# Rows of four tokens per partition, D x made in the merge, and the next B and C loaded between batches, in a four-layer selective-scan and FFT network

## The chip, the cores and the metric

The kernel runs on one core of a Trainium2 chip, as one launch that holds a whole four-layer network. The metric is the device time of one execution in microseconds (us). Everything in the network is in 32-bit floats but a part of the feed-forward layers, which this change does not touch.

## What is computed

The input x is an image batch of (4, 64, 64, 96): four images, 4096 tokens each, 96 channels. Four layers follow one another, each adding to a running x. Layers 0 and 1 are selective state-space layers over images ("SS2D"), and they hold the change; layers 2 (linear attention and a feed-forward part) and 3 (a filter in the frequency domain and a feed-forward part) do not take part in it. Layer 0, cut to what matters:

```
xz = gn(x) @ in_proj_w.T;  xc, z = split(xz)             # 192 channels each
xc = silu(depthwise_conv3x3(xc))
idx, inv = scan orders                                    # four orders of the 4096 tokens
xs = [xc in the order idx[k] for k in 0..3]
dt, B, C = projections of xs[k];  delta = softplus(dt)
h_t = h_(t-1) * exp(delta_t * A) + delta_t * u_t * B_t    # 16 states for each channel
y_t = sum over states of h_t * C_t
out_y = y + Ds[k] * xs[k]
y_restored = [out_y[k] in the order inv[k]]
w = softmax(small net on each token's position)           # one weight per token and order
y = sum_k w[k] * y_restored[k]
y = layernorm(y) * silu(z);  return y @ out_proj_w.T
```

Layer 1 has the same core with four fixed directions (rows, columns, and both backwards) and no weights w, so that its D terms are a plain sum over k; a feed-forward part follows it. "D x" below is the term of Ds times x summed over the four orders, with the weights w in layer 0.

## The kernel before, in words

**Stages.** The class `Stream` (lines 312 to 1089) does layer 0 and the scans of layer 1. It works on eight batches in turn, q = 0 to 7: the four images of layer 0 ("L0"), then the four of layer 1 ("L1"). A batch has 16 segments: four orders (kd = 0 to 3) of 4096 tokens, cut into four pieces of 1024. A segment has 24 groups, six blocks of 32 channels (cb) by four groups of four states (sg); a group lays 32 channels x 4 states on the 128 partitions, and 1024 tokens along the free axis.

**The scan**, `run`, lines 989 to 1084. The order of its instructions is written out by hand, two groups to a slot. For a group, DVE multiplies u by B (`enter`, L893) and runs the recurrence (`recur`, L900); POOL multiplies the states by C (`leave`, L910); PE sums the states into y (`collect`, L921); ACT makes the decays exp(delta A) (`decay`, L888). u is spread over the partitions by PE (`spread_u`, L880) into a single PSUM buffer, once for each cb. B and C of a segment lie in the tile `bc`, filled by eight loads of 512 KB from DRAM (`load_states`, L865); the loads for the segment that follows are issued in the last two slots of a segment, as its tile parts come free. The delta rows of a cb come by `load_dt` (L871). Beside the groups, the next segment is prepared in small steps (`prepare`, lines 761 to 859), which a helper, `Weave`, places between the PE and ACT work of the slots.

**From channels to tokens.** After each odd cb the y of 64 channels and 1024 tokens is turned (`turn`, lines 955 to 987): four PE transposes of 128x128 (L962), then an ACT copy (L965), three times a segment. In these transposes `yc` is the stationary operand, loaded by a weight load, and the identity moves. When the third is done the segment's rows go to the DRAM tensor `y_tok` of that kd: by eight indirect stores of POOL in the scan order (L974; L0, kd 0 and 1), by one store of SP (L983; L0, kd 2 and 3, and L1, even kd), or by two strided stores of SP (L986; L1, odd kd). Partition p then holds token p of each 128, so that one row of 192 channels, 768 bytes, is contiguous in DRAM.

**Between batches**, `side_by_side` (lines 678 to 706) writes out two stages together: the `merge` of the batch before and the `front` of a batch to come: in the seam ahead of batch q, the merge of q-1 and the front of q+1. Both are written as threads (generators) that name an engine and an assumed time before each step; `Plan` (lines 146 to 198) puts the steps in the order in which a simple model would start them, "ahead" being a priority. `Rings` (lines 204 to 224) say how many buffers of a tile there are: a thread waits till one has been given back. This fixes the order on each engine's queue. SP takes its DMAs strictly in order, and so does POOL with its gathers and multiplications; a DMA that must wait for its tile holds all that are queued behind it.

- *front* (lines 351 to 535): loads of x (L369) and its halo (L381), group norm, the input projection (L429, L445), the convolution on PE in four strips of 1024 tokens (L482), Silu (L494); then 12 transposes a strip (L509; `xc` is stationary) and ACT copies (L512) give `y_rows`, which SP stores as `x_tok` (L520). POOL multiplies the rows by D's weights, in L0 a table by token, `weight_x`, loaded from DRAM by L502, in L1 one row (L523 and L525, 128x1536 elements), and SP stores the product as `dx_tok` (L529). The product's tile, `sp_z`, has one buffer.
- *merge* (lines 538 to 676): for each of eight chunks of 512 tokens, loads of y of the four kd (SP L575; POOL gathers L580 for kd 2 and 3 of L0, four a chunk and kd), a load of `dx` (L550, one buffer), DVE sums (L603 in L0 with w, L607 in L1), statistics (L617, L618), normalisation (L625 to L630), eight transposes back to channels (L638) into one PSUM buffer, ACT's scale and shift (L647), DVE's multiplication by z (L651); then in L0 the output projection (L663) and the new x (L668, L672), in L1 the store of y (L657).

The start does two fronts without a merge. Ahead of q=7 the seam has a merge alone, and after q=7 there is a last merge alone.

Of the kernel before, what the change touches and what calls it, by code (L numbers as in the profile page):

```python
# [23 lines left out]
L = HW * HW  # L24
# [215 lines left out]
class Layer:  # L240


    def __init__(self, s, a, pre, x_in):
# [35 lines left out]
        if self.ordered:  # L279
            self.weight_x = k.t(s.dram, [L, DI], pre + "weight_x", bufs=1)  # L280
            ds = k.load(s.seg, a[pre + "Ds"], "ds")
            for c in range(NCH):
                turned = k.t(s.ps, [ND, CH], "m")
                for j in range(CH // 128):
                    nc.tensor.transpose(
                        turned[:, j * 128 : (j + 1) * 128], s.fuse[:, c * (CH // 128) + j, :], k.ident
                    )
                part = k.t(s.core, [ND, CH], "h", bufs=4)
                nc.vector.tensor_copy(part, turned)
                ps = k.t(s.ps_t, [128, 2, CH], "t")  # L290
# [10 lines left out]
                nc.sync.dma_start(  # L301
                    self.weight_x[c * CH : (c + 1) * CH, :].rearrange("(j p) d -> p j d", p=128),
                    rows.rearrange("p a (b d) -> p (a b) d", d=DI),
                )
        else:
            ds = k.t(s.core, [128, ND, DI], "h", bufs=4)
            nc.sync.dma_start(ds, a[pre + "Ds"].unsqueeze(0).to_broadcast([128, ND, DI]))
            self.weight_x = k.t(w, [128, DI], pre + "weight_x")
            nc.vector.tensor_reduce(self.weight_x, ds.rearrange("p k d -> p d k"), AX.X, ALU.add)


class Stream:
# [38 lines left out]
    def front(self, bt, plan, rings, first=None):  # L351
# [7 lines left out]
        bt.x_tok = k.t(self.dram, [L, DI], "x_tok")  # L359
        bt.dx_tok = k.t(self.dram, [L, DI], "dx_tok", bufs=3)  # L360
# [105 lines left out]
        def convolve(s, st):  # L466
# [30 lines left out]
            to = lambda v: v[s * SEG : (s + 1) * SEG, :].rearrange("(j p) d -> p j d", p=128)  # L497
            dx = yield from take(self.seg, [128, 2, SEG], "sp_z", 1)
            dxs = dx.rearrange("p h t -> p (h t)")[:, : SEG // 128 * DI].rearrange("p (j d) -> p j d", d=DI)
            if lay.ordered:  # L500
                yield "SP", 0.1
                nc.sync.dma_start(dxs, to(lay.weight_x))  # L502
            rows = yield from take(self.tmp, [128, 2, 4, DI], "y_rows", 1)
            two = yield from take(self.ps_t, [128, 2, CH], "t", 2)
            one = yield from take(self.ps, [128, CH], "m", 1)
            for blk, ps in enumerate((two[:, 0, :], two[:, 1, :], one)):
                yield "PE", 1.2
                for t in range(4):
                    nc.tensor.transpose(ps[:, t * 128 : (t + 1) * 128], xc[blk][:, t * 128 : (t + 1) * 128], k.ident)  # L509
                yield "ACT", 0.8  # L510
                for half in range(2):
                    nc.scalar.copy(  # L512
                        rows[:, :, :, half * C + blk * GC : half * C + (blk + 1) * GC],
                        ps.rearrange("p (t h j d) -> p h j t d", h=2, j=2, d=GC)[:, half],
                    )
            give(two, one, *xc)
            del two, one, ps, xc
            flat = rows.rearrange("p j t d -> p (j t) d")
            yield "SP", 0.1
            nc.sync.dma_start(to(bt.x_tok), flat)  # L520
            yield "POOL", 3.5
            if lay.ordered:
                nc.gpsimd.tensor_mul(dxs, dxs, flat)  # L523
            else:
                nc.gpsimd.tensor_mul(dxs, flat, lay.weight_x.unsqueeze(1).to_broadcast([128, SEG // 128, DI]))  # L525
            give(rows)
            del rows, flat
            yield "SP", 0.1
            nc.sync.dma_start(to(bt.dx_tok), dxs)  # L529
            yield "none", 2.5  # L530
            give(dx)
            del dx, dxs
# [5 lines left out]
    def merge(self, bt, plan, rings):  # L538
# [1 line left out]
        k, nc, tmp, lay = self.k, self.nc, self.tmp, bt.lay  # L540
        take, give = rings.take, rings.give
        T = CH // 128
        rows_of = lambda v, n: v[n * CH : (n + 1) * CH, :].rearrange("(j p) d -> p j d", p=128)
        cols_of = lambda n: slice(n * CH, (n + 1) * CH)
        got = {}

# [13 lines left out]
        rings.parts("rows", [whole[:, i, : T * DI].rearrange("p (j d) -> p j d", d=DI) for i in range(2)])  # L560
        whole = k.t(self.seg, [C, 2, SEG], "xs")
        rings.parts("z", [whole[:, i].rearrange("p (h t) -> p h t", h=2) for i in range(2)])

        def fetch(kds):
            if kds[0]:
# [22 lines left out]

        def sums():
            for n in range(NCH):  # L590
                plan.add(load(("dx", n), tmp, [128, T, DI], "dx", 1, rows_of(bt.dx_tok, n)))
            for n in range(NCH):
                acc = yield from take(self.core, [128, T, DI], "hc", 3)
                yield lambda: ("dx", n) in got
# [27 lines left out]
        def finish(n, acc, mv):  # L622
# [21 lines left out]
            yield "ACT", 1.4  # L644
            for half in range(2):
                g, b = lay.ln_g[:, half : half + 1], lay.ln_b[:, half : half + 1]
                nc.scalar.activation(yt[:, half], ps[:, half], AF.Identity, bias=b, scale=g)  # L647
            yield lambda: ("z", n) in got
            z = got.pop(("z", n))
            yield "DVE", 1.1  # L650
# [24 lines left out]

        yield from plan.together([fetch((0, 1)), fetch((2, 3)), sums()])

    def side_by_side(self, ahead, behind=None, flush=None):


        k, nc = self.k, self.nc
        plan, rings = Plan(), Rings(k)
        self.ended, self.idle = False, None

        def ending():

            yield "none", 1.2
            if flush:
                flush()
            self.idle = k.t(self.ps_y, [128, CH], "y")  # L690
            self.ended = True
            yield "PE", 4.0

        def fill():
            if self.idle is not None:
                data = self.layers[0].diag.rearrange("p h t c -> p (h t c)")[:, :384]
                nc.tensor.matmul(self.idle[:GC, :384], self.zeros, data, start=True, stop=True)

        plan.fill = fill
        if behind:  # L700
# [254 lines left out]
    def turn(self, seg, pair, yc):  # L955

        k, nc = self.k, self.nc
        if pair == 0:
            seg.rows = self.spare()[:, : SEG // 128 * DI].rearrange("p (f t d) -> p f t d", f=2, d=DI)
        ps = k.t(self.ps, [128, CH // 128, 128], "m")  # L960
        for j in range(CH // 128):
            nc.tensor.transpose(ps[:, j, :], yc[:, j * 128 : (j + 1) * 128], k.ident)  # L962
        self.put += 0.66
        yield
        nc.scalar.copy(seg.rows[:, :, :, pair * 64 : (pair + 1) * 64], ps.rearrange("p j (f d) -> p f j d", f=2))  # L965
        if pair == 2:
# [13 lines left out]
                    )  # L980
            elif seg.bt.lay.ordered or seg.kd % 2 == 0:
                at = self.start(seg)
                nc.sync.dma_start(to[at : at + SEG, :].rearrange("(j p) d -> p j d", p=128), rows)  # L983
            else:
                for w in range(2):
                    nc.sync.dma_start(self.by_columns(to, seg, w), rows[w * HW : (w + 1) * HW])  # L986
# [2 lines left out]
    def run(self):  # L989
# [15 lines left out]
        with k.tc.manual_schedule():  # L1005
# [16 lines left out]

            for n, (seg, cb, sg) in enumerate(slots):
                follows = seg.next
                if first_of(slots[n]):
                    q = batches.index(seg.bt)
                    if q:
                        self.side_by_side(batches[q + 1 : q + 2], batches[q - 1], flush)
                    before = []
                    seg.bt.y_tok = [k.t(self.dram, [L, DI], f"y_tok{kd}") for kd in range(ND)]  # L1030
                    self.spread_u(seg, 0)
# [41 lines left out]
                if cb == NCB - 1 and follows:  # L1073
# [3 lines left out]
                if cb == NCB - 1 and follows:  # L1077
# [14 lines left out]
def fusion_weights(k, s, a, fuse):  # L1092
# [871 lines left out]

def constants():
    c = {}
    for name, order in zip(("scan_idx", "scan_inv"), scan_orders()):
        c[name] = order.reshape(ND, L // 128, 128).transpose(2, 0, 1).astype(np.uint32)
# [4 lines left out]
    c["coords"] = np.stack([r.ravel(), (np.arctan2(dy, dx) / f(math.pi)).ravel()])  # L1973

    one = np.kron(np.eye(GC), np.ones((1, GS)))
    c["spread"] = np.tile(one, (C // GC, 1))
# [105 lines left out]
```

## Time and profile before

| | |
|---|---|
| median of 3 runs | 16010.31 us (16001.02 to 16012.46) |
| the profiled execution | 15991.09 us |
| its span, first to last instruction | 15989.3 us, mean granted PE clock 0.87 |
| scans and seams (`Stream`) | to about 12,880 us of the span |
| start, to the first enter | 395.4 us |
| seams ahead of q = 1 to 7 (last leave to first enter) | 174.9, 173.7, 174.5, 178.6, 164.5, 162.9, 101.0 us |
| last merge | about 104 us, from 12,776 |
| one batch | 1356 (the last) to 1425 us (the first) |

The page of the profile gives, for each engine, its busy time; then the span in 40 slices, each digit a busy share in tenths; the DMA queues; the chain of work that ended last; and groups of instructions, each with its line, its engine, the tiles it writes and reads, its count, busy time, mean duration, and the idle time of its engine ahead of it with what ended that idle time. A window is a stretch of the span for which the same busy times are asked. PEld is PE's loading of weights, which lies beside its matmuls; SPq lines are DMAs that SP issues, with the time at which each issue began. The trace also has each DMA packet with its size and time; the DMA share is the busy time of the packets over that of the core's 16 DMA engines.

### The profile page before, as it was taken

To read this page: it belongs to the slowest core of one execution; us is meant where nothing else is said; L and a number is where in the kernel's file an instruction comes from. 1 tells how busy PE (TensorE), PEld (TensorE's weight loads), DVE (VectorE), ACT (ScalarE), POOL (GpSimd) and SP (SyncE) were. 2 spreads that over 40 slices of the span, in tenths; PEclk is the share of its full clock that TensorE was granted. 3 is DMA by queue.
4 is the path that set the end of the run, shared out by engine and by line. 5 is a ranking of instruction groups with operands and counts; after the bars stand their busy time and mean duration, and the time that the engine had idled before them with its cause. 6 is when DMAs were issued, how large, how long until landed. Compare 5 with 4: busy or idle time off the path is not lost. (4 is left out here: it accounts for less than half of the span.)

```text
span 15989.3 us, 190160 instructions
## 1 busy us (share of the span) xinstructions
PE 13629.1 (85%) x70689; PEld 4868.9 (30%) x70689; DVE 12884.4 (81%) x9642; ACT 8295.0 (52%) x14192; POOL 9763.9 (61%) x4881
## 2 busy tenths in 40 slices
PE   7888888888888888888878887888888879998877
PEld 3222322232222222222222222222222234443344
DVE  1989798979897989799979997999899965565555
ACT  3656465646564656465555555656466522332334
POOL 0788688868886888677747774777577720000123
PEclk8888888888888888888888888888888889998878
DMA  3333533353335333533353334333433320000132
GB/s 98 113 105 119 161 106 104 118 162 105 113 110 153 107 114 108 154 109 118 106 151 120 105 119 150 111 115 108 145 110 121 104 65 18 18 11 14 39 82 70
DMA packets 883162, 1662.26 MB, mean 104 GB/s; under 512 B 103078, under 2 KB 551339, under 8 KB 878460
## 3 DMA queue, kind: packets, MB, share of 16 engines
q1 hardware_dynamic: 845372, 1574.54, 31.8%
q0 software_dynamic: 36864, 75.55, 1.6%
q8 instruction: 560, 9.18, 0.2%
q14 instruction: 366, 3.00, 0.1%
HBM read 1295.03 MB, written 354.75 MB: 103 GB/s over the span
## 5 line engine op out<-in xcount | busy, mean ns | idle before, releaser
L910 POOL TENSOR_TENSOR hc<-h,bc 128x1024 f32<-128x1024 f32 x3072 | 7186.2, 2358 | 2386.9 <-DVE h L900 1935.1
L900 DVE TENSOR_TENSOR_SCAN h<-da,state,t 128x1024 f32<-128x1024 f32 x2304 | 5271.0, 2328 | 14.1 <-ACT da L888 10.5
L921 PE MATMUL y<-hc,gather_y 128*32 128x512 f32 x12288 | 4295.0, 691 | 700.2 <-POOL hc L910 534.5
L893 DVE TENSOR_TENSOR t<-u,bc 128x1024 f32<-128x1024 f32 x3072 | 3599.8, 1217 | 1023.0 <-PE u L880 899.4
L888 ACT ACTIVATE da<-dts,L_A_logs 128x1024 f32<-128x1024 f32 x3072 | 3487.8, 1147 | 746.2 <-DMA dts<-dt_dram 476.1
L880 PE MATMUL u<-dtu,spread 32*128 32x512 f32 x3072 | 1897.9, 745 | 377.8 <-DVE t L893 370.4
L944 PE MATMUL y<-L_diag,zeros 96*32 96x256 f32 x5218 | 1747.8, 465 | 0.0
L900 DVE TENSOR_TENSOR_SCAN h<-da,t 128x1024 f32<-128x1024 f32 x768 | 1711.8, 2268 | 17.6 <-ACT da L888 16.8
L921 PEld LDWEIGHTS y<-hc,gather_y 128*32 128x32 f32 x12288 | 804.3, 117 | 2499.8 <-issue 1280.2
L849 ACT COPY dt<-m 96x512 f32<-96x512 f32 x512 | 297.1, 580 | 1588.1 <-PE m L844 1588.1
L812 PE MATMUL m<-xs,proj 96*128 96x512 f32 (+1 forms) x2048 | 1016.8, 619 | 115.9 <-ACT dt L821 62.7
L880 PEld LDWEIGHTS u<-dtu,spread 32*128 32x128 f32 x3072 | 603.7, 217 | 1460.0 <-issue 1106.8
L944 PEld LDWEIGHTS y<-L_diag,zeros 96*32 96x32 f32 x5218 | 617.4, 132 | 1283.6 <-issue 1156.4
L1265 POOL MEMSET padp<- 128x2448 f32 x32 | 68.6, 2144 | 1481.9 <-PE d L1305 1376.1
L1341 DVE SCALAR_TENSOR_TENSOR hcv<-padv,taps,hcv 128x2048 f32<-128x2048 f32 x384 | 902.2, 2350 | 13.4
L1305 PE MATMUL d<-padp,diag 32*32 32x512 f32 x25600 | 885.7, 601 | 2.0 <-ACT hcp L1320 2.0
L844 PE MATMUL m<-sp_z,ident 96*96 96x512 f32 x1024 | 534.9, 604 | 190.1 <-ACT sp_z L838 189.9
L804 POOL TENSOR_TENSOR dtu<-sp_z,dtu 96x1024 f32<-96x1024 f32 x256 | 604.2, 2360 | 72.6 <-ACT dtu L802 70.2
L816 ACT ACTIVATE sp_z<-m,L_dtb 96x512 f32<-96x512 f32 x512 | 349.3, 682 | 544.4 <-PE m L812 529.5
L1305 PEld LDWEIGHTS d<-padp,diag 32*32 32x32 f32 x25600 | 483.5, 103 | 370.6 <-issue 197.9
L965 ACT COPY spare<-m 128x512 f32<-128x512 f32 x384 | 225.4, 587 | 706.3 <-PE m L962 706.3
L812 PEld LDWEIGHTS m<-xs,proj 96*128 96x128 f32 (+1 forms) x2048 | 321.8, 177 | 821.9 <-issue 314.8
(275 smaller groups left out, 15523.6 us busy)
## 6 DMA issues: line engine op xcount, KB each, us to landing
bc<-bc_dram SPq DMA_DIRECT2D x1024, 512.0 KB
dts<-dt_dram SPq DMA_DIRECT2D x768, 512.0 KB
dt_dram<-dt SPq DMA_DIRECT2D x256, 384.0 KB
y_tok<-spare SPq DMA_DIRECT2D x64, 768.0 KB
dt<-y_tok SPq DMA_DIRECT2D x128, 384.0 KB
z_t<-z_rows SPq DMA_DIRECT2D x64, 384.0 KB
x_tok<-y_rows SPq DMA_DIRECT2D x32, 768.0 KB
dx_tok<-sp_z SPq DMA_DIRECT2D x32, 768.0 KB
```

The lines of the kernel that those rows point to most:

```text
L804: rest = lambda half: nc.gpsimd.tensor_add(r[:, half], z[:, half], r[:, half])
L812: nc.tensor.matmul(ps, proj[:, src, to], xs[:, src, cols], start=src == 0, stop=src == 1)
L844: nc.tensor.matmul(ps, k.ident[:C, :C], term[:, half, cols], start=at == 0, stop=at == 2)
L880: self.nc.tensor.matmul(seg.u[:, cols], self.spread[rows, :], seg.dtu[rows, half, cols], start=True, stop=True)
L888: self.nc.scalar.activation(da, seg.dts[cb], AF.Exp, scale=seg.bt.lay.neg_a[:, seg.kd, g : g + 1])
L893: self.nc.vector.tensor_mul(gr.t, gr.seg.u, self.bc[:, 0, gr.sg, :])
L900: self.nc.vector.tensor_tensor_scan(gr.h[:, order], gr.da[:, order], gr.t[:, order], start, op0=ALU.mult, op1=ALU.add)
L910: self.nc.gpsimd.tensor_mul(gr.hc, gr.h, self.bc[:, 1, gr.sg, :])
L921: nc.tensor.matmul(seg.y[at : at + GC, :], self.gather_y, gr.hc[:, part * CH : (part + 1) * CH], start=gr.sg == 0, stop=gr.sg == NSG - 1, ...
L944: self.nc.tensor.matmul(gr.seg.y[at : at + GC, :256], self.zeros, gr.seg.bt.lay.diag.rearrange("p h t c -> p (h t c)")[:, :256], start=Fal ...
L1305: nc.tensor.matmul(pc[i][j * 32 : (j + 1) * 32, :], diag[mine, ON_PE.index(t), tap, :], pad[mine, j * 8 + dy : j * 8 + dy + 8, dx : dx + H ...
L1341: nc.vector.scalar_tensor_tensor(to, win, wt, to, op0=ALU.mult, op1=ALU.add)
```

## The change

There are three parts. Line numbers here are those of the kernel before.

1. *Rows of fours.* Partition p holds the four tokens 4p to 4p+3 of each 512 instead of token p of each 128. For this the transposes take every fourth column of their operand (L509 always; L962 in L0, and in L1 for even kd), and the stores and loads of `weight_x`, `x_tok` and `y_tok` in that layout are of 3072 contiguous bytes to a partition instead of four times 768. The constants for the orders and the positions are permuted to match. When the merge turns chunks back to channels, ACT's L647 reads PSUM in the permuted order and writes in the plain one. The strided stores of L1's odd kd and the loads of `x_tok` for the scans (`fetch`) stay as they are.
2. *D x in the merge.* The front no longer loads `weight_x`, multiplies, or stores `dx_tok`. The merge loads `x_tok` where it loaded `dx_tok`, in L0 also `weight_x`, and POOL multiplies the two, a chunk of 128x768 at a time, ahead of the sums. `x_tok` now has three DRAM buffers.
3. *B and C late.* The eight loads of `bc` and the first of the delta rows for a new batch are no longer issued in the last slots of the batch before, but by a thread of the seam, `states`: the first after 50 of the plan's us, the others 4 apart.

```diff
             for blk, ps in enumerate((two[:, 0, :], two[:, 1, :], one)):
                 yield "PE", 1.2
                 for t in range(4):
-                    nc.tensor.transpose(ps[:, t * 128 : (t + 1) * 128], xc[blk][:, t * 128 : (t + 1) * 128], k.ident)
+                    nc.tensor.transpose(ps[:, t * 128 : (t + 1) * 128], xc[blk][:, t::4], k.ident)
...
-            if lay.ordered:
-                yield "SP", 0.1
-                nc.sync.dma_start(dxs, to(lay.weight_x))
...
+            to = bt.x_tok[s * SEG : (s + 1) * SEG, :].rearrange("(j p t) d -> p j (t d)", j=2, t=4)
             yield "SP", 0.1
-            nc.sync.dma_start(to(bt.x_tok), flat)
-            yield "POOL", 3.5
-            if lay.ordered:
-                nc.gpsimd.tensor_mul(dxs, dxs, flat)
-            else:
-                nc.gpsimd.tensor_mul(dxs, flat, lay.weight_x.unsqueeze(1).to_broadcast([128, SEG // 128, DI]))
+            nc.sync.dma_start(to, rows.rearrange("p j t d -> p j (t d)"))
...
-            nc.sync.dma_start(to(bt.dx_tok), dxs)
...
-        rows_of = lambda v, n: v[n * CH : (n + 1) * CH, :].rearrange("(j p) d -> p j d", p=128)
+        rows_of = lambda v, n: v[n * CH : (n + 1) * CH, :].rearrange("(p j) d -> p j d", j=T)
...
+        def times_d(n):
+            x = yield from take(tmp, [128, T, DI], "dx", 1)
+            yield "SP", 0.1
+            nc.sync.dma_start(x, rows_of(bt.x_tok, n))
+            weight = lay.weight_x
+            if lay.ordered:
+                weight = yield from take(None, None, "weight", 2)
+                nc.sync.dma_start(weight, rows_of(lay.weight_x, n))
+            yield "none", 3.0
+            yield "POOL", 1.8
+            if lay.ordered:
+                nc.gpsimd.tensor_mul(x, x, weight)
+                give(weight)
+            else:
+                nc.gpsimd.tensor_mul(x, x, weight.unsqueeze(1).to_broadcast([128, T, DI]))
+            got["dx", n] = x
...
             for n in range(NCH):
-                plan.add(load(("dx", n), tmp, [128, T, DI], "dx", 1, rows_of(bt.dx_tok, n)))
+                plan.add(times_d(n), 1)
...
-                nc.scalar.activation(yt[:, half], ps[:, half], AF.Identity, bias=b, scale=g)
+                to, v = yt[:, half].rearrange("c (p j) -> c p j", j=T), ps[:, half].rearrange("c (j p) -> c p j", j=T)
+                nc.scalar.activation(to, v, AF.Identity, bias=b, scale=g)
...
+        def states():
+            for at in range(2 * NSG):
+                yield "none", 50.0 if at == 0 else 4.0
+                yield "SP", 0.1
+                self.load_states(seg, *divmod(at, NSG))
+            self.load_dt(seg, 0)
...
+        fours = seg.bt.lay.ordered or seg.kd % 2 == 0
         for j in range(CH // 128):
-            nc.tensor.transpose(ps[:, j, :], yc[:, j * 128 : (j + 1) * 128], k.ident)
+            v = yc[:, j::4] if fours else yc[:, j * 128 : (j + 1) * 128]
+            nc.tensor.transpose(ps[:, j, :], v, k.ident)
...
-                nc.sync.dma_start(to[at : at + SEG, :].rearrange("(j p) d -> p j d", p=128), rows)
+                to = to[at : at + SEG, :].rearrange("(f p t) d -> p f (t d)", f=2, t=4)
+                nc.sync.dma_start(to, seg.rows.rearrange("p f t d -> p f (t d)"))
...
                 follows = seg.next
+                near = follows and follows.bt is seg.bt
...
-                        self.side_by_side(batches[q + 1 : q + 2], batches[q - 1], flush)
+                        self.side_by_side(batches[q + 1 : q + 2], batches[q - 1], flush, seg)
...
-                elif sg == 0 and follows:
+                elif sg == 0 and near:
                     self.load_dt(follows, 0)
...
-                    if cb == NCB - 1 and follows:
+                    if cb == NCB - 1 and near:
                         self.load_states(follows, 0, gr.sg)
```

More of the change, by code (lines that the diff above doesn't have):

```diff
@@ L301, in __init__ @@
                 nc.sync.dma_start(
-                    self.weight_x[c * CH : (c + 1) * CH, :].rearrange("(j p) d -> p j d", p=128),
-                    rows.rearrange("p a (b d) -> p (a b) d", d=DI),
+                    self.weight_x[c * CH : (c + 1) * CH, :].rearrange("(p j) d -> p (j d)", j=4),
+                    rows.rearrange("p a e -> p (a e)"),
                 )
@@ L358, in front @@
         x = lay.x_in[:, bt.b, :]
-        bt.x_tok = k.t(self.dram, [L, DI], "x_tok")
-        bt.dx_tok = k.t(self.dram, [L, DI], "dx_tok", bufs=3)
+        bt.x_tok = k.t(self.dram, [L, DI], "x_tok", bufs=3)
         bt.z_t = k.t(self.dram, [C, 2, L], "z_t", bufs=3)
@@ L496, in convolve @@
             del two, one, ps
-            to = lambda v: v[s * SEG : (s + 1) * SEG, :].rearrange("(j p) d -> p j d", p=128)
-            dx = yield from take(self.seg, [128, 2, SEG], "sp_z", 1)
-            dxs = dx.rearrange("p h t -> p (h t)")[:, : SEG // 128 * DI].rearrange("p (j d) -> p j d", d=DI)
-            if lay.ordered:
-                yield "SP", 0.1
-                nc.sync.dma_start(dxs, to(lay.weight_x))
             rows = yield from take(self.tmp, [128, 2, 4, DI], "y_rows", 1)
@@ L517, in convolve @@
             del two, one, ps, xc
-            flat = rows.rearrange("p j t d -> p (j t) d")
+            to = bt.x_tok[s * SEG : (s + 1) * SEG, :].rearrange("(j p t) d -> p j (t d)", j=2, t=4)
             yield "SP", 0.1
-            nc.sync.dma_start(to(bt.x_tok), flat)
-            yield "POOL", 3.5
-            if lay.ordered:
-                nc.gpsimd.tensor_mul(dxs, dxs, flat)
-            else:
-                nc.gpsimd.tensor_mul(dxs, flat, lay.weight_x.unsqueeze(1).to_broadcast([128, SEG // 128, DI]))
-            give(rows)
[L527 to L532, printed above, removed]
+            nc.sync.dma_start(to, rows.rearrange("p j t d -> p j (t d)"))
+            yield "none", 2.5
+            give(rows)
+            del rows
         works = [work for s, st in enumerate(strips) for work in (project(s, st), convolve(s, st))]
@@ L562, in merge @@
         rings.parts("z", [whole[:, i].rearrange("p (h t) -> p h t", h=2) for i in range(2)])
+        whole = k.t(self.seg, [128, 2, SEG], "sp_z")
+        rings.parts("weight", [whole[:, i, : T * DI].rearrange("p (j d) -> p j d", d=DI) for i in range(2)])
+        def times_d(n):
[14 more added lines that the diff above has]
+            got["dx", n] = x
         def fetch(kds):
@@ L676, in merge, with side_by_side @@
         yield from plan.together([fetch((0, 1)), fetch((2, 3)), sums()])
-    def side_by_side(self, ahead, behind=None, flush=None):
+    def side_by_side(self, ahead, behind=None, flush=None, seg=None):
         k, nc = self.k, self.nc
@@ L697, in fill @@
                 nc.tensor.matmul(self.idle[:GC, :384], self.zeros, data, start=True, stop=True)
+        def states():
[4 more added lines that the diff above has]
+            self.load_dt(seg, 0)
         plan.fill = fill
+        if seg:
+            plan.add(states())
         if behind:
@@ L1072, in run @@
                 self.leave(now[0])
-                if cb == NCB - 1 and follows:
+                if cb == NCB - 1 and near:
                     self.load_states(follows, 1, now[0].sg)
@@ L1076, in run @@
                 self.leave(now[1])
-                if cb == NCB - 1 and follows:
+                if cb == NCB - 1 and near:
                     self.load_states(follows, 1, now[1].sg)
@@ L1966, in constants @@
     c = {}
-    for name, order in zip(("scan_idx", "scan_inv"), scan_orders()):
-        c[name] = order.reshape(ND, L // 128, 128).transpose(2, 0, 1).astype(np.uint32)
+    idx, inv = scan_orders()
+    tiles = lambda v: v.reshape(-1, L // 128, 128).transpose(2, 0, 1)
+    fours = lambda v: v.reshape(-1, NCH, 128, 4).transpose(2, 0, 1, 3).reshape(128, -1, L // 128)
+    c["scan_idx"] = np.concatenate([fours(idx[:2]), tiles(idx[2:])], axis=1).astype(np.uint32)
+    c["scan_inv"] = fours(inv).astype(np.uint32)
     f = np.float32
@@ L1972, in constants @@
     r = np.minimum(np.sqrt(dy**2 + dx**2), f(2.0))
-    c["coords"] = np.stack([r.ravel(), (np.arctan2(dy, dx) / f(math.pi)).ravel()])
+    coords = np.stack([r.ravel(), (np.arctan2(dy, dx) / f(math.pi)).ravel()])
+    c["coords"] = coords.reshape(2, NCH, 128, 4).swapaxes(2, 3).reshape(2, L)
     one = np.kron(np.eye(GC), np.ones((1, GS)))
```

## Prediction

> **What bounds the kernel now.** I read the totals first, then the slices of the span, then the costliest groups, then windows cut at the seams between batches.
>
> ```profile
> PE 13629.1 (85%) x70689; PEld 4868.9 (30%) x70689; DVE 12884.4 (81%) x9642; ACT 8295.0 (52%) x14192; POOL 9763.9 (61%) x4881
> ...
> DVE  1989798979897989799979997999899965565555
> ...
> DMA  3333533353335333533353334333433320000132
> ...
> L900 DVE TENSOR_TENSOR_SCAN h<-da,state,t 128x1024 f32<-128x1024 f32 x2304 | 5271.0, 2328 | 14.1 <-ACT da L888 10.5
> ...
> L893 DVE TENSOR_TENSOR t<-u,bc 128x1024 f32<-128x1024 f32 x3072 | 3599.8, 1217 | 1023.0 <-PE u L880 899.4
> ```
>
> The 81% of DVE is a mean over two regimes. Slices 1 to 32 are the scans (to about 12,880 us): DVE has 8s and 9s, with a dip wherever the DMA row rises to 5; those dips are the seams. A segment needs 24 x (1.217 + 2.328) = 85.1 us of DVE, and the undisturbed ones, from first enter to first enter, take 85.4: DVE bounds the scan, and what holds DVE up there is PE, whose spread of u it awaits for 899 us in all. The rest of the program, 12,880 to 15,989, is not touched.
>
> Windows at the first L0 seam, the first seam of L1 merges with an L1 front (q=5), the merge-only seam (q=7), the last merge and the last batch (columns: stretch, length, busy PE, PEld, DVE, ACT, POOL, granted clock, DMA share, GB/s):
>
> ```profile
> 1820.00:1995.00 175.00, 130.32 (x1157) 59.04 (x1156) 100.15 (x276) 66.91 (x100) 81.25 (x69) 0.86 0.76 221
> 8179.00:8344.00 165.00, 111.25 (x1108) 54.56 (x1106) 80.83 (x172) 62.80 (x97) 13.46 (x5) 0.80 0.70 208
> 11319.00:11420.00 101.00, 62.69 (x174) 22.43 (x172) 64.42 (x144) 18.96 (x30) 0.39 (x1) 0.74 0.83 241
> 12776.00:12880.00 104.00, 60.30 (x172) 22.29 (x170) 65.27 (x150) 15.81 (x27) 0.24 (x1) 0.73 0.79 223
> 11420.00:12776.00 1356.00, 1197.98 (x3635) 375.07 (x3635) 1292.94 (x768) 811.31 (x1281) 1035.56 (x444) 0.88 0.36 111
> ```
>
> In the batch DVE is busy 1293 of 1356 us and DMA has room (0.36). In the seams no engine is full; DMA is the nearest to it. The seams sum to 1,130 us (175 x 3, 179, 165, 163, 101) and the last merge to 104: the stage in which parts two and three of the change work.
>
> **Part one, D x in the merge.** Per seam with a front, four 768-KB stores of dx_tok go (4,096 packets of 768 B; the trace's packet records have a median of 36 ns for these, so 4,096 x 36 / 16 engines = 9.2 us of DMA time). The loads only change their name: the merge reads x_tok where it read dx_tok, and in L0 weight_x where the front read it. POOL's four muls of 128x1536 (3.45 us) become eight of half the size, about 1.75 us each by halving: no saving in sum. What SP was held by goes too:
>
> ```profile
> 1898.92 0.38 SPq L529 DMA_DIRECT2D dx_tok<-sp_z  x1
> ...
> 1903.72 0.38 SPq L502 DMA_DIRECT2D sp_z<-L_weight_x  x1
> ```
>
> The load of the next weights overwrites the tile whose store must land first, and SP, in order, stood until 1903.7 (3.8 us of the gap); the same happens at 1958 (4 us). Behind it stand the merge's loads. The price: the chunk's mul now stands between its load and its first sum.
>
> ```profile
> 1840.04 1.41 DVE L603 SCALAR_TENSOR_TENSOR hc<-dt,fuse,dx 128x192 f32<-128x192 f32 x4 [22.80 <-DMA dx<-dx_tok]
> ```
>
> DVE waited 22.8 us for the first dx; afterwards it waits for the load and 1.75 us of POOL. On POOL (in order) the four gathers of kd 3 of a chunk, 1.25 us each, queue behind a mul that waits for two loads, and DVE's sums of kd 2 and 3 wait for them. POOL is busy 81 of 175 us, so in mid-seam this is covered by the front's work; at the end of an L0 seam chunks finish 6.6 to 8 us apart, while a ring of one buffer makes sum, load (3.7 us from issue to landing at 1841), mul and sum 7 to 11 us. Without the cover: at most 3 us for each of the last four chunks, 12 us a seam.
>
> **Part two, fours.** 768-B packets become 3072 B in the stores of x_tok and y_tok and in the merge's loads: 20,000 to 24,000 in a seam. No packet of this size is in the trace; between 2048 B (84 ns) and 4096 B (159) lies 121 ns, against 4 x 36 = 144. Saving: 5,100 to 6,000 x 23 / 16 = 7.4 to 8.6 us of DMA time a seam. [...] The trace has 21.3 B/ns at 768 and 24.4 at 2048, so I keep the row.
>
> Its cost is in PE's transposes: L962 in `turn` (96 of 128 segments) and L509 in the front read the stationary operand at every fourth element. The nearest strided weight load is L1733, 64 elements apart:
>
> ```profile
> L962 PEld LDWEIGHTS m<-ident,yc x1536: 137/141/231, 458.2 to 12779.1; 128*128 128x128 f32 x192
> ...
> L1733 PEld LDWEIGHTS m<-w,ph x512: 185/222/258, 15252.9 to 15667.5; 97*64 97x64 f32 x171
> ```
>
> (min/median/max ns.) With half the columns L1733 takes 222 ns where L962 takes 141. If the excess over a plain load goes with columns, a strided load of 128 is about 0.11 us longer (four to a `turn`, +0.43 us); at the most 0.17 (+0.7); at the least nothing, as loads lie beside the matmul before. Three turns a segment; DVE was late for u at cb 2 on 99 of 128 segments and at cb 4 on 121, the places behind a turn: 96 x (99 + 121)/128 = 165 turns on the path, so 0 to 115 us, 71 by L1733. That row also differs in tile and in its matmul, and the turn has something else ahead of it (PE idled 219 us for ACT before L962). I take 5 us, near the lower end, for the likeliest case and carry 71 as a rival. [...] ACT's read of PSUM in L647 becomes strided by 512 B (0.774 us now): 0 to +0.77 each, 16 a merge, off the path beside a front, up to 12 us in each of two merge-only stages. POOL's muls come to these two as well, and there they meet DVE:
>
> ```profile
> 8255.60 4.04 POOL L525 TENSOR_TENSOR sp_z<-y_rows,L_weight_x 128x1536 f32<-128x1536 f32 x1 [76.47 <-ACT y_rows L512]
> ...
> 8256.17 4.28 DVE L607 TENSOR_TENSOR hc<-dx,dt 128x768 f32<-128x768 f32 x1
> ```
>
> L607 takes 0.95 us alone and 4.28 beside the mul: up to 1.75 us a chunk for half a mul.
>
> **Part three, B and C late.** Eight loads of 512 KB (1.27 us of all engines each, 128 x 159 ns / 16) and one of dts leave the batch's last slots for mid-seam. Two or three landed in the seam anyway, so +6 to +8 us of DMA time, issued 50 us in; the first loads of y and dx, which took 8.6 and 9.8 us to land, go freely. SP issues nine more DMAs (about 0.45 us, 4 us), ahead of half the merge's loads; it waits for nothing new, since the batch before has done with the tile. In q=7 the loads fall among the last three chunks where DMA is full: up to +5 us.
>
> **Sum**, against the profiled execution (15,991 us, span 15,989):
> - q=1 to 4: DMA -9 -8 +7 = -10 of 133 us of packet time, SP 8 us less held, tail up to +12: bounds -14 to +4, taken -8 each, -32.
> - q=5, 6: the same DMA, no weights, no gathers: -14 to 0, taken -10 each, -20.
> - q=7: no front, so no store of dx goes, and DMA is -7 +7; 0 (-4 to +17). Last merge: -2 (-7 to +12); its chunks are set by the store of y1 (`y<-yt` held ACT 124 us), not by dx.
> - Start, two fronts on a full PE: 96 strided loads, 0 to +10; taken +4.
> - Scan: +5.
>
> -45: 15,946. The three timed runs have a median 19 us above the profiled one, so the median becomes **15,965**.
>
> **Rivals.**
> - *Strided loads cost what L1733 says.* +71 instead of +5: 16,012, or 16,031 as a median. For: PE's u is the one thing DVE waits for. Against: the pairing of load and matmul may hide it. [...]
> - *Slower: PE's lateness turns segments into the longer pattern.* Segments have two lengths in the trace: those of the last batch take at most 85.6, those of q=4 to 6 stay at 88.8 from the third to sixth on until the seam; the granted clock toggles between 1.0 and 0.5, and the 88.8 ones have about 17 us at 0.5 against 10. A longer turn can push a batch over. Twenty of the some 55 that now take up to 86.4 are +68 on top of the rival above: 16,080, or 16,099. It decides from about four such segments on, if the loads are long.
> - *Seams gain more.* If they follow DMA and SP to the bounds (6 x -14), the start is free, and seven segments return to 85.4 (-24): 15,991 - 84 - 11 - 24 = 15,872, or 15,891.
>
> **Chances.** Forecast 0.42, seams more 0.10, strided loads 0.22, longer pattern 0.26. A measurement can tell about 0.2% (32 us) from no change. Of the forecast 0.36 lies below 15,978; of the strided case 0.19 within 32 us and 0.03 above: faster 0.46, same 0.25, slower 0.29. The range, 15,870 to 16,105, leaves out the last part of the seams case and the upper half of the longer pattern.
>
> **What would show it.** Right: seams from last leave to first enter of about 167 (L0) and 154 us; no wait of SP before a load of weights; L962's loads near 141 ns; 3072-B packets near 121 ns; segments no longer. Wrong: L962's loads at 220 ns or more with L893's wait for u up by 70 us; 88.8 in q=0 to 2 or 7; DVE waiting for POOL's mul in the tails; the first enter of a batch waiting for bc or dts.

## The result, and the profile after

The changed kernel takes 15860.68 us (median of 4 runs, 15856.05 to 15870.14) against 16010.92: a ratio of 0.9908, 95% interval 0.9891 to 0.9925. The forecast was 15,965, its range ended at 15,870: the direction was right and the size was not. The profiled execution is 129 us shorter, and 100 of these came in the scans, where the sum had +5. Profiled executions, from the last `leave` of a batch to the first `enter` of the next, in us:

| stage | before | after | difference | forecast |
|---|---|---|---|---|
| start | 395.4 | 389.0 | -6.4 | +4 |
| seams q=1 to 4 | 701.7 | 706.0 | +4.3 | -32 |
| seams q=5, 6 | 327.4 | 311.4 | -16.0 | -20 |
| seam q=7 | 101.0 | 99.7 | -1.3 | 0 |
| scans of L0 | 5677 | 5661 | -16 | +5 for both |
| scans of L1 | 5574 | 5490 | -84 | |
| last merge and all behind it | 3213.1 | 3202.6 | -10.5 | -2 |

The page's line of busy times, and the rows that answer to L900 and L893 of before:

```profile
PE 13616.6 (86%) x70721; PEld 4897.8 (31%) x70721; DVE 12867.0 (81%) x9642; ACT 8291.1 (52%) x14188; POOL 9781.6 (62%) x4913
...
L918 DVE TENSOR_TENSOR_SCAN h<-da,state,t 128x1024 f32<-128x1024 f32 x2304 | 5271.5, 2329 | 11.5 <-ACT da L906 8.7
...
L911 DVE TENSOR_TENSOR t<-u,bc 128x1024 f32<-128x1024 f32 x3072 | 3601.2, 1218 | 895.2 <-PE u L898 780.8
```

DVE's work is the same to 0.2%; its wait for u fell by 119 us (899.4 to 780.8). So the scans gained where they were expected to lose. Windows at the same four seams (columns as before):

```profile
1815.20:1991.10 175.90, 139.12 (x1161) 62.41 (x1160) 100.14 (x275) 66.98 (x100) 83.58 (x72) 0.84 0.70 222
8129.00:8284.00 155.00, 109.71 (x1100) 52.65 (x1098) 79.01 (x171) 58.91 (x94) 15.46 (x9) 0.82 0.71 227
11184.00:11284.00 100.00, 63.35 (x184) 23.15 (x181) 64.43 (x144) 17.55 (x29) 17.03 (x9) 0.79 0.85 276
12657.00:12761.00 104.00, 59.81 (x186) 23.02 (x184) 69.88 (x157) 15.81 (x27) 22.38 (x12) 0.78 0.75 235
```

In the first, the DMA share fell from 0.76 to 0.70 (133 to 123 us of packet time, as summed), and the seam did not get shorter: the time of DMA's packets was not what set its length.

**What the grid is.** In the trace the granted clock is 1.0 or 0.5 and changes only on a grid of 3.413 us that runs through the whole program. A segment of 85.4 us is 25 of its windows (85.33), one of 88.8 is 26 (88.75). Windows cut on that grid, in the same segment of q=5 (the 13th), first before, then after (it is the first of kd 3, whose own turns are contiguous in both, so that it only keeps the place on the grid that kd 2 left it; length, busy PE, PEld, DVE, ACT, POOL, granted clock, DMA share, GB/s):

```profile
9434.05:9437.46 3.41, 3.41 (x15) 1.04 (x12) 3.41 (x4) 1.98 (x4) 3.41 (x3) 1.00 0.00 0
9437.46:9440.87 3.41, 1.76 (x4) 0.57 (x4) 3.41 (x3) 3.39 (x4) 2.24 (x1) 1.00 0.45 154
9440.87:9444.29 3.42, 3.42 (x5) 1.16 (x4) 2.04 (x1) 3.41 (x6) 2.36 (x1) 0.50 0.00 0
9444.29:9447.70 3.41, 3.41 (x8) 0.56 (x8) 1.97 (x2) 1.51 (x4) 0.01 (x1) 0.50 0.00 0
9447.70:9451.11 3.41, 3.41 (x10) 1.07 (x8) 3.41 (x3) 0.00 (x0) 3.01 (x2) 0.50 0.00 0
```

```profile
9366.28:9369.70 3.42, 3.42 (x18) 1.21 (x14) 3.42 (x3) 0.91 (x3) 3.42 (x2) 1.00 0.00 0
9369.70:9373.11 3.41, 2.91 (x12) 0.85 (x11) 3.41 (x3) 2.89 (x3) 3.09 (x2) 1.00 0.00 0
9373.11:9376.52 3.41, 2.26 (x5) 0.86 (x6) 2.91 (x2) 3.38 (x5) 2.35 (x1) 1.00 0.46 154
9376.52:9379.94 3.42, 3.42 (x13) 0.97 (x12) 1.78 (x2) 3.42 (x6) 0.69 (x1) 1.00 0.00 0
```

PE has the same idle time here (it waits for ACT's part of `prepare`). Before, it lies in one window, which is busy for 1.76 of 3.41, and the next three are granted 0.5; PE is late, and DVE waits for u. After, it is split over two windows of 2.91 and 2.26, and no low clock follows. DVE's enters of the two segments show the price (before, then after; the bracket is the wait):

```profile
9445.73 2.37 DVE L893 TENSOR_TENSOR t<-u,bc 128x1024 f32<-128x1024 f32 x2 [2.82 <-PE u L880]
...
9463.16 2.36 DVE L893 TENSOR_TENSOR t<-u,bc 128x1024 f32<-128x1024 f32 x2 [3.98 <-PE u L880]
```

```profile
9378.16 2.37 DVE L911 TENSOR_TENSOR t<-u,bc 128x1024 f32<-128x1024 f32 x2 [2.14 <-PE u L898]
...
9392.89 2.36 DVE L911 TENSOR_TENSOR t<-u,bc 128x1024 f32<-128x1024 f32 x2 [1.38 <-PE u L898]
```

The delay keeps the next segment at the same point of the grid, so that the long form repeats until something shifts it. Among the first 15 segments of a batch, those of 88.2 to 89.3 us in q=4 to 6 are 10, 10 and 12 before; 1, 4 and 0 after (q=7: none before, 4 after).

What runs in a window counts too, not only how long PE is busy. In the scans of before, 107 windows at full clock had PE busy for 0.70 to 0.85 of the time with the spread of u (L880) taking at least 0.4 of the window: 104 of them were followed by a window at 0.5, and of the other 297 of the same busy share none (after: 109 of 112, and 1 of 339). Windows at 0.5 in which PE was busy for 0.85 or more were followed by another at 0.5 in all 285 cases with that much spread, and in none of the 339 in which it took less than 0.1 (after: 294 of 294, and none of 346). So a low clock that meets the spread lasts through it, and that is when DVE waits. The spread's matmuls read 32 partitions where the other matmuls of the scans read 96 or 128; whether this has a part in it, no run tested.

### The profile page after: what moved, and what is told of

Its sections match the earlier page's. It is cut to its first block, busy times and chain, and to the rows that moved or that the text cites. A ratio compares the mean times of both kernels' runs of the same rounds, so it can differ in the third digit from the quotient of the medians.

```text
span 15859.9 us, 190275 instructions
## 1 busy us (share of the span) xinstructions
PE 13616.6 (86%) x70721; PEld 4897.8 (31%) x70721; DVE 12867.0 (81%) x9642; ACT 8291.1 (52%) x14188; POOL 9781.6 (62%) x4913
## 5 line engine op out<-in xcount | busy, mean ns | idle before, releaser
L911 DVE TENSOR_TENSOR t<-u,bc 128x1024 f32<-128x1024 f32 x3072 | 3601.2, 1218 | 895.2 <-PE u L898 780.8
L962 PE MATMUL y<-L_diag,zeros 96*32 96x256 f32 x5218 | 1736.9, 463 | 0.0
L962 PEld LDWEIGHTS y<-L_diag,zeros 96*32 96x32 f32 x5218 | 617.2, 132 | 1274.9 <-issue 1114.7
```

The source lines that it names most:

```text
L911: self.nc.vector.tensor_mul(gr.t, gr.seg.u, self.bc[:, 0, gr.sg, :])
L962: self.nc.tensor.matmul(gr.seg.y[at : at + GC, :256], self.zeros, gr.seg.bt.lay.diag.rearrange("p h t c -> p (h t c)")[:, :256], start=Fal ...
```

## The experiments

Theory A: the clock's grid sets the scans, and the strided `turn`, a little longer, moves segments off the long form; what the seams gained comes from one part alone. Rivals are in the expectations; their absolute times are for the chip of the result, where before takes 16,010. The experiments ran in four groups of four kernels, each group on another chip of the same kind; each ratio is against runs of the kernel before on the same chip. Single profiles differ from their medians by up to 45 us, and on the first three of these chips an L0 seam takes 190 to 218 us, with or without the change, against 174 to 179 on the chip of the result; I conclude nothing from L0 seams there.

### Which part carries the scans

The changed kernel with a contiguous `turn`:

```diff
-            v = yc[:, j::4] if fours else yc[:, j * 128 : (j + 1) * 128]
+            v = yc[:, j * 128 : (j + 1) * 128]
```

> The changed kernel, with the transposes of `turn` reading contiguous columns again; stores and loads stay those of the fours, so the rows of y land in another order than the reference's. Theory A (the granted clock changes on a grid of 3.413 us, segments lock to 25 or 26 of its windows, 85.4 or 88.8 us, and the strided turn, 0.09 us longer, tips segments of L1 out of the longer lock): the recoveries at kd 2 of q=5 and q=7 are lost, some 12 segments of 3.3 us, about 15,900. Theory B (only the point on the grid at which a seam releases a batch decides): within 15 us of 15,861. Theory C (strided turns make the whole gain of the scans): about 15,960.

0.9979 (0.9961 to 0.9997). L1's scans take 5627 us, with 9, 10, 13 and 13 long segments: the gain of the scans is gone, as C put it (15,960 is 0.997 of 16,010; A's 15,900 is 0.993): all of it hangs on this line.

The opposite, the kernel before with only that line strided:

> The kernel before, with only the transposes of `turn` strided (L0, and even kd of L1); nothing else, so the rows of y land in another order than the reference's. Theory A: q=4, 5 and 6 leave the 88.8-us lock during kd 2, six or seven segments each, about 16,010 - 65 = 15,945. Theory B: 16,010 within 20 us. Theory C: about 15,910.

0.9957 (0.9938 to 0.9975), as A put it; L1's scans 5488, as after the change (5490), while its L1 seams are those of before (328 us).

The kernel before, with no stride but one transpose more:

```diff
+        fours = seg.bt.lay.ordered or seg.kd % 2 == 0
+        for j in range(1 if fours else 0):
+            nc.tensor.transpose(ps[:, j, :], yc[:, j * 128 : (j + 1) * 128], k.ident)
```

> The kernel before, with one of the four transposes of `turn` done once more in the segments that the change makes strided: PE 0.11 us longer a turn without any stride. Theory A: as the strided turn, about 15,945, since it is the length that counts. Theory B: 16,010 within 20 us. If the stride does something other than lengthen the turn: also 16,010.

0.9938 (0.9909 to 0.9968); L1's scans 5486. Length does it; the stride is not needed. (Whether the added work counts by shifting PE's idle time or by filling the window is not told apart here.) Work added to the engine that DVE waits for made the kernel faster.

A delay at the seams instead, four idle matmuls of PE ahead of each batch:

> The kernel before, with four idle matmuls of PE (0.3 to 0.6 us each) at the end of each seam, so that each batch starts 1.2 to 2.5 us later. Theory A in its strict form, that the turn alone tips the lock: 16,010 + 8 to 17. Theory B: the batches' patterns change, anywhere from -120 to +60, and the phase at which the first segments start tells which.

0.9992 (0.9975 to 1.0009), L1's scans 5633. Within a few segments the batches fall back into the long form (13, 13, 6, 14 segments). This is one delay, of 2 to 3 us as the L1 seams show it; all profiles together say more. Of the 24 L1 batches profiled with the contiguous turn and the filler of before (before twice, e1, e5, e7, e13), which start all over the grid, 23 have six long segments or more; of the 24 with the even turns strided or lengthened and the odd ones as they were (the change twice, e2, e3, e4, e8), 3 have. So theory B falls as the cause of the gain, though the start has a hand in single batches: q=7 of before has no long segment.

### Both kernels again, and the parts taken out one by one

> The kernel before, unchanged, for its profile on the chip on which the next three run. Theory A: most segments of q=4 to 7 at 88.8 us (26 windows of the clock's grid), and the total within 0.3% of the runs of the kernel before beside it.

0.9999 (0.9976 to 1.0022); L1's scans 5591, L1 seams 329.2.

> The changed kernel, unchanged, on this chip. Theory A: its segments of q=4 to 7 are mostly 85.4 to 85.7 long, its L1 seams 7 to 10 us shorter than those of the kernel before and its L0 seams the same within 5; the ratio 0.985 to 0.995, more than half of it from the scans.

0.9922 (0.9901 to 0.9943); L1's scans 5484, L1 seams 312.8. The result holds on a second chip.

The changed kernel with its rows, packets and transposes as before:

> The changed kernel without its fours: D x in the merge and the late B and C stay, all rows go as 768-byte packets, no transpose is strided. Theory A: the scans go back to the kernel before's (within 0.3%), the seams of L1 lose most of their gain, the last merge too: 0.995 to 1.003. If the seams' gain is that of parts two and three (D x and the late loads), and the scans' gain comes from the point at which seams release them: 0.988 to 0.994.

1.0004 (0.9982 to 1.0027); L1's scans 5617 with 42 long segments, L1 seams 314.8. The fours carry the scans, as A said; but A also had the L1 seams lose most of their gain, and of that the fours carry 2 us for two at the most.

With D x in the front again:

> The changed kernel with D x made in the front and stored as before (in fours); the fours and the late B and C stay. Theory A: the scans keep their gain, since `turn` is strided: 0.988 to 0.996, and seams with a front are 0 to 8 us longer than the changed kernel's. If D x in the merge was what released the batches at a better point: 0.997 to 1.003.

0.9940 (0.9920 to 0.9959); L1's scans 5455, L1 seams 330.3: D x in the merge carries the seams (17.5 us for two, a little over what A allowed). The late loads, which this kernel has too, left these seams as before_again had them.

With B and C early again:

```diff
-                near = follows and follows.bt is seg.bt
+                near = follows
-                        self.side_by_side(batches[q + 1 : q + 2], batches[q - 1], flush, seg)
+                        self.side_by_side(batches[q + 1 : q + 2], batches[q - 1], flush)
```

> The changed kernel with the loads of B, C and the first delta rows of a batch issued in the last slots of the batch before again. Theory A (the length of `turn` sets the scans, D x in the merge the L1 seams, late loads little): 0.989 to 0.996 of the kernel before, L1 seams within 4 us of the changed kernel's. If the late loads make the seams' gain: seams of L1 back to 164 and the merge-only seam 3 to 8 us shorter than 100.

0.9955 (0.9932 to 0.9978); L1 seams 297.7 for the two, against 309 to 315 in the three kernels with late loads on the same chip, and the merge-only seam 97.6. Where D x is in the merge, the late loads cost, in these seams; neither theory had expected that. The whole is nevertheless not faster than the changed kernel was, because L1's scans came out at 5514, with 16 long segments in q=5 and 7: the pattern again.

### The clock itself

One transpose more in the turns that stayed contiguous:

> The changed kernel, with one transpose done once more in the turns that stayed contiguous (odd kd of L1), so that all turns are 0.09 to 0.11 us longer than in the kernel before. Theory A: the 88.8-us stretches at kd 1 of L1, some 10 segments of 3.3 us, end sooner; 0.002 below the changed kernel's ratio of 0.992, if those segments answer as the even ones do. If the stride is what counts: 0.992 as the changed kernel.

0.9944 (0.9921 to 0.9967), L1's scans 5514 (5484 and 5490 with the change alone, on other chips): a miss. A longer turn is no cure by itself; it moves the pattern, and where the even kd were helped these were not.

More filler in the scans. Filler is the matmuls of zeros (L944) that `keep_busy` puts between PE's steps, up to an assumed busy time for each half slot:

```diff
-        half_slot, least, one = 3.6, 2.1, 0.48
+        half_slot, least, one = 3.6, 2.6, 0.48
```

> The changed kernel with more idle matmuls in the scans: `keep_busy` fills each half slot to 2.6 assumed us of PE work instead of 2.1, one matmul of 256 columns (0.23 to 0.48 us) more in most half slots. Theory A, mechanism: a window of 3.413 us in which PE is busy for less than about 0.55 is followed by windows at half clock, and these make DVE wait for u. With fewer such windows, segments fall towards 81 us (24 pairs of DVE work without the waits): 0.955 to 0.985. If the half clock is not set by PE's idle time, or PE's time is what lacks: 0.992 to 1.01.

0.9876 (0.9837 to 0.9915); mean granted clock 0.921 (0.869 before), L1's scans 5433, with no long segment among the first 15 of any L1 batch. The clock rose and the waits for u fell (675.4 us, against 822.0 in the run before this one, on the same chip), but the gain is smaller than A's 0.955 to 0.985: L1's segments came to 82 to 86 us, not towards 81.

> The same with 3.1 us of 3.6: two matmuls more in most half slots. Theory A: no window under 0.55 left in a segment, clock 1.0, 0.945 to 0.98; but where the added work itself makes PE late for u, waits return and the ratio lies above that of 2.6.

0.9994 (0.9979 to 1.0009), clock 0.935, L1's scans 5508. The clock rises further and the time is lost again: DVE waits 804.6 us for u, against 675.4 at 2.6. In the 4 us ahead of a spread, PE ran 0.98 us of filler on average, against 0.40 at 2.6, so that the added matmuls stand in its way; that this is the whole of the loss is not shown.

### Do the parts add up?

> The kernel before with only `keep_busy` at 2.6. Theory A (the change's gain in the scans is a shift on the clock's grid, so a steadier clock takes its place): 0.988 to 0.992, within 0.004 of the changed kernel with 2.6 once the 15 to 30 us of the L1 seams and the start are taken off. If the length of `turn` gains by itself: at 0.995 or above.

The kernel before, its filler alone changed: 0.9853 (0.9826 to 0.9881), a larger gain than A's 0.988 to 0.992. L1's scans take 5411 us. Without one strided read it gains more than the change did.

> The kernel before with D x made in the merge and nothing else (no fours, early B and C). Theory A: L1 seams at 297 to 303 us for the two (329 before), L1 scans as before (5574 to 5634): 0.997 to 1.001. If fours are needed for the seams' gain: L1 seams above 312.

0.9937 (0.9917 to 0.9957). L1 seams 301.3 (329 before), L1's scans 5589 as before. The ratio is lower than A allowed: start, L1 seams and last merge account for some 40 us of the 95. In the profile, which is 26 us slower than the median, L0's scans are 28 us under the first profile's; the rest is not settled.

> The changed kernel with part three undone (B and C loaded in the last slots of the batch before) and `keep_busy` at 2.6. Theory A: the scans of 2.6 and the shorter L1 seams of early loads add up: 0.983 to 0.988 of the kernel before. If they do not add, because early loads disturb the ends of batches: 0.988 to 0.992.

0.9819 (0.9795 to 0.9843), 15712.25 us, just past A's 0.983: the fastest of all with the next one, below both kernels. D x in the merge, early B and C, filler 2.6. The clock row of before, then of this run with its row of enters (for before, see L893 in the prediction):

```profile
PEclk8888888888888888888888888888888889998878
```

```profile
PEclk9999899999999999999989998999899999998888
...
L911 DVE TENSOR_TENSOR t<-u,bc 128x1024 f32<-128x1024 f32 x3072 | 3597.4, 1216 | 780.4 <-PE u L898 665.9
```

Its L1 scans (5425) are no better than those of the kernel before with the same filler (5411): with a steadier clock the strided turn gained nothing.

> As the changed kernel with early loads and `keep_busy` at 2.6, but at 2.8. Theory A: between the results of 2.6 and 3.1, since the added work begins to hold up u: 0.987 to 0.996; if idle windows still decide at 2.6, below its result.

0.9825 (0.9800 to 0.9850): no different from 2.6, where A had expected 0.987 to 0.996. At 2.8 the added filler shows no cost yet.

## Why the prediction was wrong, step by step

**What bounds the scan: wrong.** "24 x (1.217 + 2.328) = 85.1" added durations that overlap on DVE. The starts of before show it:

```profile
9476.42 2.34 DVE L893 TENSOR_TENSOR t<-u,bc 128x1024 f32<-128x1024 f32 x2
...
9483.16 2.33 DVE L893 TENSOR_TENSOR t<-u,bc 128x1024 f32<-128x1024 f32 x2
...
9489.90 1.20 DVE L893 TENSOR_TENSOR t<-u,bc 128x1024 f32<-128x1024 f32 x1
```

Where nothing is waited for, four groups take 13.47 us, so 24 take 80.8. A segment of 85.4 holds 4.3 us of waits for u, one of 88.8 7.6. PE's lateness was a part of every segment, and its clock decided how much.

**The scan, "+5": the step that failed, in sign and in size.** The strided load takes longer by itself:

```profile
L983 PEld LDWEIGHTS m<-ident,yc x1536: 137/209/231, 451.9 to 12659.4; 128*128 128x128 f32 x192
```

The median of all went from 141 to 209 ns, but three of the four loads of a turn begin while the transpose before runs, which hides most of the 68 ns: one transpose follows another after 120 ns instead of 109, and four take 0.746 us instead of 0.656. That is +0.09 us a turn, not the 0.43 that L1733 gave: 165 x 0.09 = 15 us by my own count of turns on the path. What failed is the next thought, that a longer turn can only delay u. PE had idle time (the prediction's last window has it busy for 1198 of 1356 us), and its clock goes by windows of 3.413 us: with 0.09 us more a turn, L1's scans, which hold 84 of the 100 us, left the long form (0.11 us of plain transpose did the same). The few us of L0's scans are within what single profiles vary by. The rival "longer pattern" had the mechanism and the wrong sign; its figures were wrong too (a long segment has 27.3 us at 0.5, a short one 20.5).

**L1 seams, "-20": near in size, wrong in reason.** I gave it to DMA and SP. The trace of before, at the head of the q=5 seam:

```profile
8200.33 0.96 DVE L607 TENSOR_TENSOR hc<-dx,dt 128x768 f32<-128x768 f32 x1 [23.98 <-DMA dx<-dx_tok]
...
8202.40 4.83 DVE L373 BATCH_NORM_STATS2 gn_stats<-da 96x6 f32<-96x512 f32 x8
```

and after:

```profile
8142.73 1.28 DVE L372 BATCH_NORM_STATS2 gn_stats<-da 96x6 f32<-96x512 f32 x2 [16.16 <-DMA da<-x]
8144.19 1.28 DVE L372 BATCH_NORM_STATS2 gn_stats<-da 96x6 f32<-96x512 f32 x2 [0.19 <-DMA da<-x]
...
8149.83 0.96 DVE L614 TENSOR_TENSOR hc<-dx,dt 128x768 f32<-128x768 f32 x1 [1.22 <-POOL dx L568]
```

Before, the first sum stands ahead of the front's statistics on DVE and holds them while it waits for dx. After, the plan knows that dx comes later (a load and POOL's mul) and puts the statistics first. They end some 9 us earlier in the seam, the convolutions follow 8 to 22 us earlier, and the seam is 6 to 10 us shorter, with D x alone 13. That D x in the merge does it is shown by the runs; that it is this order on DVE, and not the stores of dx that go with it, is read from the trace, as no run changes the order alone. I had shown the wait of 22.8 us in L0 and not asked what was queued behind it. The fours' packets did what they should (a median of 121 ns in the seams, as interpolated; the start of before had 128 such packets, also at 121, which I had missed; that is 25.4 B/ns, against 21.3 at 768 bytes), and it was worth 2 us at the most.

**L0 seams, "-32": wrong.** The statistics start about 10 us earlier here too, but the lead is lost at the third strip, whose halo is loaded by SP behind the merge's DMAs:

```profile
1902.97 1.60 DVE L420 TENSOR_SCALAR halo<-halo,gn 96x128 f32<-96x128 f32 x1 [9.31 <-DMA halo<-in_x]
...
1922.13 0.31 DVE L420 TENSOR_SCALAR halo<-halo,gn 96x64 f32<-96x64 f32 x1 [11.95 <-DMA halo<-in_x]
```

In the q=1 seam the third strip's Silu comes 114.1 us in, against 108.3 before. With D x alone it comes at 110.6, so part of it stands behind the late B and C. That freeing SP of the weight loads would shorten these seams was argued, not shown; it did not.

**Late B and C, "+6 to +8 us of DMA time", taken as hidden: wrong.** With D x in the merge they cost 6 to 9 us in each L1 seam, by the run that put them back; with D x in the front (and the fours) these seams took what they took before. Nothing in the runs shows what they bring.

**Start, q=7, last merge.** Start -6.4 instead of +4, which is no proof of a gain: in single profiles the start of before took 389.2 to 398.6 us, that of the change up to 397.0. The last merge alone, to its last product, went from 101.2 to 94.4 us, at my lower bound; but 101.2 is the highest of the profiles with the rows of before and no change in the merge (95.0 to 101.2), and the changed kernel repeated gave 94.6. L647's strided read of PSUM takes 772 ns against 774: free. POOL's mul cost 1.8 us a chunk, as halved.

**What stays open:** why D x alone reached 0.9937, and what sets the weight of a matmul in the clock's windows. That the change is worth more on one chip than on another is not shown: the gain was 0.0092 on one and 0.0078 on another, and the intervals overlap.

## What to carry to other kernels

Where PE has idle time and another engine waits for it, look at the granted clock before pricing PE's work: here 0.09 us more in a step that recurs went with 84 us less in L1's scans, and such a gain belongs to no edit: a steadier clock replaced it (5411 us with more filler alone, 5425 with the strided turn too). Check a bound by the distance between starts, not by a sum of durations. For a wait at the head of an in-order queue, ask first what is queued behind it.

## What the runs showed of the hardware

- The granted clock was 1.0 or 0.5 and moved on a grid of 3.413 us, in the profiles of before and after. In the scans of before, of the windows at full clock, every one in which PE was busy for less than 0.4 was followed by one at 0.5 (118 of 118), from 0.40 to 0.50 27 of 45, from 0.50 to 0.55 147 of 158, from 0.55 to 0.70 10 of 231, from 0.70 to 0.85 104 of 404, above that 2 of 1472. PE's busy share alone thus does not decide: in all 114 of these between 0.55 and 0.85 the spread of u took 0.34 of the window or more. A window half busy was enough in most cases: 174 of 203 from 0.40 to 0.55.
- In the scans of before a low clock lasted one, two or three windows (165, 102 and 142 times; 12 times four or five), and the segments locked to the grid: ten in a row take 26 windows in q=4 of before (88.4 to 89.0 us), ten 25 in q=7 (85.0 to 85.4).
- A weight load at a stride of 16 bytes took 209 ns by its record, against 141 without, and one transpose followed another after 120 ns instead of 109.
